# Edge counts of a graph network's scatter by a row DMA and ScalarE instead of TensorE transposes

## The chip, the cores and the metric

The kernel runs on one core of a Trainium2 chip. The metric is the device time of one execution in microseconds (us); shown for the kernel before are nine timed runs and one profiled execution. The engines are called as the profile calls them: PE (TensorE matmuls), PEld (TensorE weight loads), DVE (VectorE), ACT (ScalarE), POOL (GpSimd) and SP (SyncE, which here only issues DMAs).

## The reference

One layer of a message-passing network on 6250 nodes of 128 features and 100000 edges, the edges sorted by destination. All is f32.

```python
msg_in = jnp.concatenate([node_features[row], node_features[col]], axis=-1)
h = jax.nn.relu(msg_in @ Wm1 + bm1)
h = jax.nn.relu(h @ Wm2 + bm2)
messages = h @ Wm3 + bm3
agg = jax.ops.segment_sum(messages, col, num_segments=num_nodes)
count = jax.ops.segment_sum(jnp.ones((messages.shape[0],), messages.dtype), col, num_segments=num_nodes)
agg = agg / jnp.clip(count, 1.0)[:, None]
node_in = jnp.concatenate([node_features, agg], axis=-1)
upd = jax.nn.relu(node_in @ Wn1 + bn1) @ Wn2 + bn2
return node_features + upd
```

`row` is `src`, `col` is `dst`; the result is `_layernorm(x + layer(x))`. The count of edges that end in each node divides the sum.

## The kernel before, in words

**Tables (L335-L350).** The first layer is linear in the two gathered rows, so `x @ Wm1` is computed once a node and kept in DRAM: `atab` (source half, f32) and `btab` (destination half, as three bf16 terms whose sum is the f32 value). For each block of four 128-node tiles, `turn` transposes x on PE and copies it on ACT (L267), `a_table` multiplies (L232), copies (ACT L241) and stores by SP (L242). `b_table`, three blocks behind, multiplies, rounds on ACT (L249), subtracts on DVE (L250), rounds on POOL or, late, on ACT (L252, L254), subtracts again (L255) and stores (L256). At block 6 `starts` and at 7 and 8 `columns` make the edges' index columns. `x_part` makes `x @ Wn1` of the first half for the end (L316 to L320). SP, ACT and POOL each issue DMAs; the order of PE is the program's, that of DVE and ACT is the program's only from L368 until iteration 6 of the loop, and elsewhere the planner's, by priorities and its own costs.

**The loop over 196 groups of 512 edges (L532-L586).** At step i: `fetch` of group i (POOL issues four indirect DMAs that gather rows of `atab`, L412, into one of four `ag` buffers; SP issues four loads of `btab` rows, L418, into one of four `bw` buffers); every second step ACT issues two loads `db` of destinations (L361); DVE makes one-hot matrices `oht` and `oh` (L433, L436). Then PE does, in this order: `add_up` of group k = i-6 (six transposes L489), `first_layer` of group i-2 (16 transposes of `ag` L449, 8 matmuls of `bw` with `oht` L455, all into the two PSUM banks `ph`; ACT applies relu, L460), `sums` of group i-5 (L478; ACT copies the result `part` out of PSUM, L481), and `second_layer` of the group before (16 matmuls L469; DVE takes the max, L471).

**The counts.** `h2` has a 257th column of ones, so column 256 of `part` (a row is one of 4 x 32 window nodes) is the number of edges. `add_up` turns `part` over: per half of 64 rows, two transposes for the 256 features and a third (c = HC) whose weights are column 256 broadcast over 128 columns, so that the counts stand in all 128 partitions of a third plane of `pt`. Four DVE adds (L494) then put the three planes onto a window of `acc`, at a node that DVE loads into a register (L497).

**After the loop (L588-L601)** the last three groups are added up, in an order written out for PE, DVE and ACT, and then a loop for edges whose windows are too narrow (L607-L633), which runs no time with these inputs.

**Nodes (L636-L766).** For 15 blocks of up to 512 nodes: `products` (`w3` times `acc`, L672; DVE adds count times bias, L674; POOL multiplies by the reciprocal of the count, L677), `hidden` (L686 to L688), `moments` (L700 to L710), `scaled` (L733, L735). PE runs `products` four blocks ahead. For the first three blocks DVE makes the reciprocal from the counts in `acc` (L666, L667); for the others one row of counts goes by DMA to a column, is inverted (L654 to L656), goes to DRAM (`rtab`, L657) and comes back broadcast (L669).

Of the kernel before, what the change touches and what calls it, by code (L numbers as in the profile page):

```python
# [19 lines left out]
P = 128  # L20
EPS = 1e-5
NONE = 16384
WN = 32
# [4 lines left out]
def kernel(  # L28
# [74 lines left out]
    rtab = dram.tile([NT * P], F32, name="rtab")  # L103
# [47 lines left out]
    with tc.tile_pool(name="prep", bufs=1) as prep, tc.tile_pool(  # L151
# [9 lines left out]
        with tc.high_priority():  # L161
            nc.scalar.dma_start(w1, wm1.rearrange("(k p) h -> p k h", p=P))
            load_rows(nc.scalar, dst_i, dst)
            load_rows(nc.gpsimd, src_i, src)
            with nc.allow_non_contiguous_dma(reason="a bias, one value a partition"):
                nc.gpsimd.dma_start(b1, bm1.rearrange("(c p) -> p c", p=P))
                nc.gpsimd.dma_start(b2, bm2.rearrange("(c p) -> p c", p=P))
                nc.gpsimd.dma_start(b3, bm3.rearrange("(c p) -> p c", p=P))
                nc.gpsimd.dma_start(bu1, bn1.rearrange("(c p) -> p c", p=P))
            nc.gpsimd.dma_start(nb2[:, 0, :], bm2.rearrange("(o h) -> o h", o=1).to_broadcast([P, H]))  # L170
# [11 lines left out]
            nc.sync.dma_start(x_sb[:N - NTF * P, NTF, :], x[NTF * P:, :])  # L182
        nc.sync.dma_start(w2, wm2.rearrange("(k p) h -> p k h", p=P))
# [35 lines left out]
        order.enter_context(tc.manual_schedule(engines={ENG.PE}))  # L219

# [22 lines left out]

        def b_table(t0):
# [5 lines left out]
            nc.vector.tensor_sub(rest[:, :m], pbt[:, :m], bt[:, :m, 0])  # L250
            if t0 < 4 * LATE:
                nc.gpsimd.tensor_copy(bt[:, :m, 1], rest[:, :m])  # L252
            else:
                nc.scalar.copy(bt[:, :m, 1], rest[:, :m])  # L254
# [80 lines left out]
        turn(0)  # L335
        for i in range(BLOCKS + BEHIND):
            if i + 1 < BLOCKS:
                turn(4 * i + 4)
            if i < BLOCKS:
                for t0 in range(4 * i, min(4 * i + 4, NT), 2):  # L340
                    a_table(t0)
            if i == INDICES:
                starts()
            if i - INDICES in (1, 2):
                columns(i - INDICES - 1)
            if i >= BEHIND:
                for t0 in range(4 * (i - BEHIND), min(4 * (i - BEHIND) + 4, NT), 2):
                    b_table(t0)
            if BLOCKS - 1 <= i < BLOCKS - 1 + len(X_BESIDE):
                whole(x_part(X_BESIDE[i - BLOCKS + 1], bank_pb, (nc.scalar, nc.scalar)))  # L350
# [445 lines left out]
```

## Time and profile before

| what | us |
|---|---|
| median of nine runs (lowest, highest) | 1430.65 (1428.83, 1433.54) |
| the profiled execution, device time | 1433.35 |
| its span, first to last instruction | 1431.6 |
| busy: PE / PEld / DVE / ACT / POOL | 1247.8 / 917.9 / 661.8 / 452.9 / 805.2 |
| tables and indices, until the first L449 | 0 to 90 |
| the loop, first L469 to the last group's | 95 to 1346 |
| nodes, first L672 to the end | 1356 to 1432 |
| one loop step, median of first L469 to first L469 | 6.32 |

A row of the profile's groups reads: line, engine, operation, tiles written <- read, shape, how many, then busy time in us and mean ns of one, then the idle time of the engine just before them and what ended most of it. A row of the timeline reads: start, duration over all, engine, line, operation, how many, and in brackets the idle time before it and what ended it. The granted TensorE clock is 0.986 of full speed over the span. DMA engines are busy 80 to 90% in the first 70 us, 40 to 50% in the loop.

### The profile page before, as it was taken

The page shows a single profiled execution, that of the slowest core. Times are in us where ns is not written, and L with a number is a line of the kernel's source. Part 1 is how long each engine was busy: PE and PEld are TensorE (multiplying, and loading weights), DVE is VectorE, ACT ScalarE, POOL GpSimd, SP SyncE. Part 2 cuts the span into 40 slices and gives each one's busy share as a digit, 9 for nine tenths or more (in the row PEclk, how much of TensorE's full clock was granted, in tenths as well). Part 3 has the DMA queues.
Part 4 walks back from the last instruction along what each step waited for, and adds up shares of the span by engine and source line. Part 5 has one row for each costly group of instructions (what it writes and reads, how often), then busy time and mean ns, then how long its engine had stood idle before and what let it go on. Part 6 is the DMA issues. An engine that isn't in the chain of part 4 may idle for free. (4 is left out here: it accounts for less than half of the span.)

```text
span 1431.6 us, 32804 instructions
## 1 busy us (share of the span) xinstructions
PE 1247.8 (87%) x11196; PEld 917.9 (64%) x11197; DVE 661.8 (46%) x2083; ACT 452.9 (32%) x1160; POOL 805.2 (56%) x859
## 2 busy tenths in 40 slices
PE   7978888988888888888888898898888888888997
PEld 6646666666666666666666666666666666666656
DVE  5733444444443434444444444444444444443577
ACT  5632222232322323232233232222323233232246
POOL 7356565656556566565665665556565565655031
PEclk9989999999999999999999999999999999999999
DMA  8855555555444444444444444444444444443053
GB/s 282 293 168 144 148 162 145 152 148 152 126 128 122 120 129 127 124 118 124 131 127 124 130 120 124 126 123 122 120 129 124 127 122 120 130 121 107 15 142 111
DMA packets 173672, 193.66 MB, mean 135 GB/s; under 512 B 30844, under 2 KB 145486, under 8 KB 173488
## 3 DMA queue, kind: packets, MB, share of 16 engines
q0 software_dynamic: 37984, 103.35, 26.4%
q1 hardware_dynamic: 106956, 61.93, 14.7%
q10 hardware_dynamic: 28564, 26.27, 6.6%
q8 instruction: 90, 1.47, 0.4%
q14 instruction: 78, 0.64, 0.1%
HBM read 168.92 MB, written 22.88 MB: 134 GB/s over the span
## 5 line engine op out<-in xcount | busy, mean ns | idle before, releaser
L412 POOL DMA_INDIRECT ag<-atab,srcT x784 | 753.0, 961 | 505.8 <-PE ph L455 294.3
L469 PE MATMUL ph<-w,h 128*128 128x256 f32 x3128 | 734.5, 388 | 1.0 <-issue 1.0
L469 PEld LDWEIGHTS ph<-w,h 128*128 128x128 f32 x3128 | 583.0, 191 | 156.2 <-issue 67.1
L460 ACT ACTIVATE h<-ph,b 128x256 f32<-128x256 f32 x782 | 306.3, 474 | 900.1 <-PE ph L455 754.4
L471 DVE TENSOR_TENSOR h<-ph,nb 128x512 f32<-128x512 f32 x391 | 269.6, 692 | 671.0 <-PE ph L449 242.3
L455 PE MATMUL ph<-oht,bw 64*128 64x128 bf16 x1564 | 126.8, 217 | 146.6 <-issue 129.8
L494 DVE TENSOR_TENSOR acc<-acc,pt 128x63 f32 x782 | 172.8, 221 | 32.1 <-PE ph L455 2.5
L455 PEld LDWEIGHTS <-bw 64*128 64x128 bf16 x1564 | 67.0, 95 | 185.4 <-issue 157.6
L449 PE MATMUL ph<-ident,ag 64*128 64x64 f32 x3128 | 132.2, 223 | 10.3 <-DVE b L382 6.5
L478 PE MATMUL pg<-h,oh 128*32 128x257 f32 x1564 | 129.3, 394 | 4.1 <-issue 2.7
L449 PEld LDWEIGHTS ph<-ident,ag 64*128 64x128 f32 x3128 | 114.3, 139 | 10.8 <-DVE b L382 6.5
L433 DVE TENSOR_SCALAR oht<-db,pbase 128x128 bf16<-128x128 int32 x392 | 104.3, 296 | 4.7 <-remote 3.0
L489 PEld LDWEIGHTS pt<-ident,part 64*128 64x128 f32 x1173 | 51.1, 136 | 65.6 <-issue 64.2
L489 PE MATMUL pt<-ident,part 64*128 64x64 f32 x1173 | 77.9, 238 | 0.0
L481 ACT COPY part<-pg 128x257 f32<-128x257 f32 x196 | 76.6, 391 | 4.0 <-PE pg L478 4.0
L436 DVE TENSOR_TENSOR oh<-iota_n,dloc 128x128 f32<-128x128 f32 x196 | 55.7, 284 | 3.4 <-PE pg L478 2.7
L677 POOL TENSOR_TENSOR agg<-total,rc 128x512 f32<-128x512 f32 (+2 forms) x15 | 16.0, 1070 | 72.0 <-DMA rcol<-acc 34.3
L478 PEld LDWEIGHTS pg<-h,oh 128*32 128x32 f32 x1564 | 31.9, 108 | 30.9 <-issue 5.7
L232 PE MATMUL pbt<-w,xT 128*128 128x256 f32 x196 | 48.6, 393 | 2.7 <-ACT bt L241 1.8
L232 PEld LDWEIGHTS pbt<-w,xT 128*128 128x128 f32 x196 | 36.6, 196 | 11.0 <-ACT bt L241 3.0
L672 PE MATMUL pmt<-acc,w 128*128 128x512 f32 (+2 forms) x60 | 26.2, 576 | 2.3 <-DVE rc L666 2.3
L252 POOL CAST bt<-rest 128x512 bf16<-128x512 f32 x18 | 12.2, 686 | 27.1 <-DVE rest L250 18.1
(110 smaller groups left out, 421.4 us busy)
## 6 DMA issues: line engine op xcount, KB each, us to landing
bw<-btab SPq DMA_DIRECT2D x782, 32.0 KB
db<-in_dst_dram ACTq DMA_DIRECT2D x194, 128.0 KB
ag<-atab,srcT POOLq DMA_INDIRECT x784
btab<-bt SPq DMA_DIRECT2D x24, 384.0 KB
atab<-bt SPq DMA_DIRECT2D x24, 256.0 KB
xd<-in_x_dram SPq DMA_DIRECT2D x12, 256.0 KB
x2tab<-xd SPq DMA_DIRECT2D x12, 256.0 KB
x_sb<-in_x_dram SPq DMA_DIRECT2D x5, 512.0 KB
```

The costliest lines, as they stand in the source:

```text
L232: nc.tensor.matmul(pbt[:, a, :], xT[:, (t0 + a) * P:(t0 + a + 1) * P], w1[:, k, :], start=True, stop=True)
L412: nc.gpsimd.indirect_dma_start(out=ag[:, j, :], out_offset=None, in_=atab[:, :], in_offset=bass.IndirectOffsetOnAxis(ap=idx[:, j:j + 1], a ...
L433: nc.vector.tensor_scalar(oht[:n, k, :], db[:n, k * P:(k + 1) * P], pb_cols[:n, k:k + 1], None, op0=ALU.is_equal)
L449: nc.tensor.matmul(phs[h][:, c, u * NQ:(u + 1) * NQ], ag[halves[h], u, c * P:(c + 1) * P], ident[halves[h], halves[h]], is_transpose=True, ...
L455: nc.tensor.matmul(phs[h][:, c, k * P:(k + 1) * P], bw[halves[h], k, c * P:(c + 1) * P], oht[halves[h], k, :], start=False, stop=True, ski ...
L460: nc.scalar.activation(h1[:, c, h * 2 * P:(h + 1) * 2 * P], phs[h][:, c, :], AF.Relu, bias=b1[:, c:c + 1])
L469: nc.tensor.matmul(ph2[:, a, :], h1[:, c, (j0 + a) * P:(j0 + a + 1) * P], w2[:, c, :], start=(c == 0), stop=(c == HC - 1))
L471: nc.vector.tensor_tensor(h2[:, j0:j0 + 2, :H], ph2, nb2.to_broadcast([P, 2, H]), op=ALU.max)
L478: nc.tensor.matmul(pg[j * WN:(j + 1) * WN, :], oh[:, j, :], h2[:, j, :], start=True, stop=True, skip_group_check=True)
L481: nc.scalar.copy(part[:n, :], pg[:n, :])
L489: nc.tensor.matmul(pt[:, c, :], rows, ident[halves[h], halves[h]], is_transpose=True, start=True, stop=True, skip_group_check=True)
L494: nc.vector.tensor_add(window, window, pts[j // 2][:, :, k:k + WB])
```

## The change

Eight parts.

1. In the loop `add_up` makes only the two feature planes on PE (four transposes a group instead of six). `sums` has ACT issue a DMA from column 256 of `part` (128 partitions, 4 bytes each) to a row `row` in one partition; a step later than before (`k = g - lag - 2`) ACT copies this row into partition 0 of the third plane. `pt` becomes one tile of two banks, set to zero once. The counts now stand in partition 0 of `acc` alone.
2. The last four groups, not three, are added up behind the loop, and these still by three transposes a half.
3. In the node stage counts are broadcast: for the first three blocks by a matmul with ones (one contraction row) and an ACT copy, for the others by loading two rows of `rtab` (reciprocals, and the counts themselves, stored by one more DMA) instead of one. `rc` has four buffers instead of six, `u` three instead of four.
4. The loads of `dst`, `src` and the biases lose their priority over the loads of x, and `dst` goes to POOL's queue.
5. ACT's order in the table stage is the program's. The first `a_table` comes before the second `turn`.
6. The second half of the late `b_table`s (`b_terms`) comes one table behind.
7. The three early loads of `db` are issued in the last blocks of the table loop, and the x parts beside them go to ACT and DVE in turn.
8. The padded copy of `dst` in DRAM (`dpad`) is written after a small tile whose stretch it overlaps.

```diff
@@ -100,7 +100,7 @@
 ...
     dpad = dram.tile([NG * GE], I32, name="dpad")
-    rtab = dram.tile([NT * P], F32, name="rtab")
+    rtab = dram.tile([2, NT * P], F32, name="rtab")
     x2tab = dram.tile([NT * P, D], F32, name="x2tab")
@@ -160,14 +160,6 @@
 ...
             nc.scalar.dma_start(w1, wm1.rearrange("(k p) h -> p k h", p=P))
-            load_rows(nc.scalar, dst_i, dst)
-            load_rows(nc.gpsimd, src_i, src)
-            with nc.allow_non_contiguous_dma(reason="a bias, one value a partition"):
-                nc.gpsimd.dma_start(b1, bm1.rearrange("(c p) -> p c", p=P))
-                nc.gpsimd.dma_start(b2, bm2.rearrange("(c p) -> p c", p=P))
-                nc.gpsimd.dma_start(b3, bm3.rearrange("(c p) -> p c", p=P))
-                nc.gpsimd.dma_start(bu1, bn1.rearrange("(c p) -> p c", p=P))
-            nc.gpsimd.dma_start(nb2[:, 0, :], bm2.rearrange("(o h) -> o h", o=1).to_broadcast([P, H]))
 ...
@@ -180,6 +172,15 @@
 ...
             nc.sync.dma_start(x_sb[:N - NTF * P, NTF, :], x[NTF * P:, :])
+        load_rows(nc.gpsimd, dst_i, dst)
+        load_rows(nc.gpsimd, src_i, src)
+        with nc.allow_non_contiguous_dma(reason="a bias, one value a partition"):
+            nc.gpsimd.dma_start(b1, bm1.rearrange("(c p) -> p c", p=P))
+            nc.gpsimd.dma_start(b2, bm2.rearrange("(c p) -> p c", p=P))
+            nc.gpsimd.dma_start(b3, bm3.rearrange("(c p) -> p c", p=P))
+            nc.gpsimd.dma_start(bu1, bn1.rearrange("(c p) -> p c", p=P))
+        nc.gpsimd.dma_start(nb2[:, 0, :], bm2.rearrange("(o h) -> o h", o=1).to_broadcast([P, H]))
         nc.sync.dma_start(w2, wm2.rearrange("(k p) h -> p k h", p=P))
 ...
@@ -217,6 +218,8 @@
 ...
         order.enter_context(tc.manual_schedule(engines={ENG.PE}))
+        turns = ExitStack()
+        turns.enter_context(tc.manual_schedule(engines={ENG.Activation}))
@@ -241,6 +244,8 @@
 ...
+        unfinished = []
         def b_table(t0):
 ...
@@ -248,6 +253,13 @@
 ...
             nc.vector.tensor_sub(rest[:, :m], pbt[:, :m], bt[:, :m, 0])
+            unfinished.append((t0, m, bt, rest))
+            if len(unfinished) > 1 or t0 < 4 * LATE:
+                b_terms()
+        def b_terms():
+            t0, m, bt, rest = unfinished.pop(0)
             if t0 < 4 * LATE:
 ...
@@ -332,13 +344,28 @@
 ...
+        def destinations(g, ng, dst_row):
+            db = ld.tile([P, 2, 2 * P], I32, name="db", bufs=3)
+            if isinstance(g, int) and g < 6:
+                nc.vector.tensor_copy(db[:, 0, :1], srcT[:, 0, :1])
+            for h in range(2):
+                edges = dst_row[:, ds(g * GE, ng * GE)].rearrange("o (s e) -> o s e", s=ng)
+                edges = edges[:, :, h * 2 * P:(h + 1) * 2 * P]
+                nc.scalar.dma_start(db[h * NQ:(h + 1) * NQ, :ng, :], edges.to_broadcast([NQ, ng, 2 * P]))
+            return [db[:, k, :] for k in range(ng)]
+        dst_row = dst.rearrange("(o e) -> o e", o=1)
+        early = []
         turn(0)
         for i in range(BLOCKS + BEHIND):
-            if i + 1 < BLOCKS:
-                turn(4 * i + 4)
-            if i < BLOCKS:
-                for t0 in range(4 * i, min(4 * i + 4, NT), 2):
-                    a_table(t0)
+            tiles = range(4 * i, min(4 * i + 4, NT), 2) if i < BLOCKS else []
+            for n, t0 in enumerate(tiles):
+                if n == (i == 0) and i + 1 < BLOCKS:
+                    turn(4 * i + 4)
+                a_table(t0)
             if i == INDICES:
 ...
@@ -346,26 +373,14 @@
 ...
                     b_table(t0)
+            if BLOCKS - 3 <= i < BLOCKS:
+                early.append(destinations(2 * len(early), 2, dst_row))
             if BLOCKS - 1 <= i < BLOCKS - 1 + len(X_BESIDE):
-                whole(x_part(X_BESIDE[i - BLOCKS + 1], bank_pb, (nc.scalar, nc.scalar)))
-        def destinations(g, ng, dst_row):
-            db = ld.tile([P, 2, 2 * P], I32, name="db", bufs=3)
-            if isinstance(g, int) and g < 6:
-                nc.vector.tensor_copy(db[:, 0, :1], srcT[:, 0, :1])
-            for h in range(2):
-                edges = dst_row[:, ds(g * GE, ng * GE)].rearrange("o (s e) -> o s e", s=ng)
-                edges = edges[:, :, h * 2 * P:(h + 1) * 2 * P]
-                nc.scalar.dma_start(db[h * NQ:(h + 1) * NQ, :ng, :], edges.to_broadcast([NQ, ng, 2 * P]))
-            return [db[:, k, :] for k in range(ng)]
-        dst_row = dst.rearrange("(o e) -> o e", o=1)
-        early = [destinations(2 * k, 2, dst_row) for k in range(3)]
-        turns = ExitStack()
-        turns.enter_context(tc.manual_schedule(engines={ENG.DVE, ENG.Activation}))
+                whole(x_part(X_BESIDE[i - BLOCKS + 1], bank_pb, (nc.scalar, nc.vector)))
+        b_terms()
+        turns.enter_context(tc.manual_schedule(engines={ENG.DVE}))
         for b in X_BEHIND:
 ...
@@ -396,7 +411,7 @@
 ...
         name="pa", bufs=1, space=PSUM
-    ) as pa, tc.tile_pool(name="pt", bufs=2, space=PSUM) as ptp:
+    ) as pa, tc.tile_pool(name="pt", bufs=1, space=PSUM) as ptp:
@@ -470,28 +485,42 @@
 ...
-        def sums(oh, h2, nt):
+        def sums(oh, h2, nt, as_row=False):
 ...
                                  start=True, stop=True, skip_group_check=True)
-            part = wk.tile([P, H + 1], F32, name="part")
+            part = wk.tile([P, H + 1], F32, name="part", bufs=3)
             nc.scalar.copy(part[:n, :], pg[:n, :])
-            return part
+            if not as_row:
+                return part, None
+            row = wk.tile([1, P], F32, name="row", bufs=3)
+            nc.scalar.dma_start(row[:, :n], part[:n, H:])
+            return part, row
+        pts = ptp.tile([P, 2, 4 * P], F32, name="pt")
+        nc.vector.memset(pts, 0.0)
+        planes = [pts[:, h, :(HC + 1) * NQ].rearrange("p (c n) -> p c n", c=HC + 1) for h in range(2)]
         def add_up(part, firsts, nt):
-            pts = [ptp.tile([P, HC + 1, NQ], F32, name="pt") for _ in range(nt // 2)]
-            for c in range(HC + 1):
-                for h, pt in enumerate(pts):
+            part, row = part
+            for c in range(HC if row is not None else HC + 1):
+                for h in range(nt // 2):
                     rows = part[halves[h], c * P:(c + 1) * P] if c < HC else part[halves[h], H:].to_broadcast([NQ, P])
-                    nc.tensor.matmul(pt[:, c, :], rows, ident[halves[h], halves[h]], is_transpose=True,
+                    nc.tensor.matmul(planes[h][:, c, :], rows, ident[halves[h], halves[h]], is_transpose=True,
                                      start=True, stop=True, skip_group_check=True)
+            if row is not None:
+                nc.scalar.copy(pts[0:1, :nt // 2, HC * NQ:(HC + 1) * NQ],
+                               row[:, :nt * WN].rearrange("o (h n) -> o h n", n=NQ))
             for j, first in enumerate(firsts):
 ...
                 k = j % 2 * WN
-                nc.vector.tensor_add(window, window, pts[j // 2][:, :, k:k + WB])
+                nc.vector.tensor_add(window, window, planes[j // 2][:, :, k:k + WB])
 ...
@@ -534,10 +563,11 @@
 ...
                 late_loads()
-                none = wk.tile([16, (NG * GE - E) // 16], I32, name="none", bufs=1)
+                none = wk.tile([16, (NG * GE - E) // 16 + 1], I32, name="none", bufs=1)
                 nc.vector.memset(none, NONE)
+                nc.sync.dma_start(dpad[E - 16:].rearrange("(p e) -> p e", p=16), none)
                 nc.sync.dma_start(dpad[:E].rearrange("(p e) -> p e", p=16), dst.rearrange("(p e) -> p e", p=16))
-                nc.sync.dma_start(dpad[E:].rearrange("(p e) -> p e", p=16), none)
             for step, after in enumerate((20, 24, 27)):
 ...
@@ -561,7 +591,7 @@
 ...
                 oht = hots.pop(g)
-            k = g - lag - 1
+            k = g - lag - 2
             if 0 <= k < NG:
 ...
@@ -577,7 +607,7 @@
 ...
                 s = st[k]
-                s["part"] = sums(s["oh"], s["h2"], s["nt"])
+                s["part"] = sums(s["oh"], s["h2"], s["nt"], as_row=k < NG - lag - 1)
 ...
@@ -587,16 +617,18 @@
 ...
             rest = (p for b in X_END for p in x_part(b, bank_p1, (nc.scalar, nc.scalar)))
-            for k in range(NG - lag, NG):
+            lasts = range(NG - lag - 1, NG)
+            for k in lasts:
                 s = st[k]
 ...
             next(rest)
-            for k in range(NG - lag, NG):
+            for k in lasts:
                 s = st[k]
-                if k + 1 < NG:
+                if lasts[0] < k + 1 < NG and "part" not in st[k + 1]:
                     st[k + 1]["part"] = sums(st[k + 1]["oh"], st[k + 1]["h2"], st[k + 1]["nt"])
                 add_up(s["part"], s["firsts"], s["nt"])
-                next(rest)
+                if k > lasts[0]:
+                    next(rest)
             assert next(rest, None) is None
 ...
@@ -652,35 +684,40 @@
 ...
         nc.sync.dma_start(rcol, acc[0:1, HC, :NT * P].rearrange("o (p n) -> o p n", n=NC))
+        nc.sync.dma_start(rtab[1:2, :], acc[0:1, HC, :NT * P])
         nc.vector.tensor_scalar_max(rcol, rcol, 1.0)
         nc.vector.reciprocal(rcol, rcol)
-        nc.sync.dma_start(rtab.rearrange("(p n) -> p n", n=NC), rcol)
-        rrow = rtab.rearrange("(o n) -> o n", o=1)
+        nc.sync.dma_start(rtab[0:1, :].rearrange("o (p n) -> (o p) n", n=NC), rcol)
+        rrows = rtab.rearrange("(o k) n -> o k n", o=1)
 ...
             w = n1 - n0
-            rc = nd.tile([P, NB], F32, name="rc", bufs=6)
+            rc = nd.tile([P, 2, NB], F32, name="rc", bufs=4)
             if b < SELF:
-                nc.vector.tensor_scalar_max(rc[:, :w], acc[:, HC, n0:n1], 1.0)
-                nc.vector.reciprocal(rc[:, :w], rc[:, :w])
+                pct = pm.tile([P, NB], F32, name="pct", tag="pmt")
+                nc.tensor.matmul(pct[:, :w], ones[0:1, :], acc[0:1, HC, n0:n1], start=True, stop=True)
+                nc.scalar.copy(rc[:, 1, :w], pct[:, :w])
+                nc.vector.tensor_scalar_max(rc[:, 0, :w], pct[:, :w], 1.0)
+                nc.vector.reciprocal(rc[:, 0, :w], rc[:, 0, :w])
             else:
-                nc.sync.dma_start(rc[:, :w], rrow[:, n0:n1].to_broadcast([P, w]))
+                nc.sync.dma_start(rc[:, :, :w], rrows[:, :, n0:n1].to_broadcast([P, 2, w]))
             pmt = pm.tile([P, NB], F32, name="pmt")
 ...
             total = nd.tile([P, NB], F32, name="total", bufs=3)
-            nc.vector.scalar_tensor_tensor(total[:, :w], acc[:, HC, n0:n1], b23, pmt[:, :w],
+            nc.vector.scalar_tensor_tensor(total[:, :w], rc[:, 1, :w], b23, pmt[:, :w],
                                            op0=ALU.mult, op1=ALU.add)
             agg = nd.tile([P, NB], F32, name="agg", bufs=5)
-            nc.gpsimd.tensor_mul(agg[:, :w], total[:, :w], rc[:, :w])
+            nc.gpsimd.tensor_mul(agg[:, :w], total[:, :w], rc[:, 0, :w])
             return agg
 ...
             w = n1 - n0
-            u = nd.tile([P, HC, NB], F32, name="u", bufs=4)
+            u = nd.tile([P, HC, NB], F32, name="u", bufs=3)
             for c in range(HC):
 ...
```

More of the change, by code (lines that the diff above doesn't have):

```diff
@@ L333 @@
         assert sorted(X_BESIDE + X_BEHIND + X_FIRST + X_END) == list(range(BLOCKS))
-        turn(0)
-        for i in range(BLOCKS + BEHIND):
-            if i + 1 < BLOCKS:
-                turn(4 * i + 4)
-            if i < BLOCKS:
-                for t0 in range(4 * i, min(4 * i + 4, NT), 2):
-                    a_table(t0)
[L342 to L349, printed above, removed]
-                whole(x_part(X_BESIDE[i - BLOCKS + 1], bank_pb, (nc.scalar, nc.scalar)))
         def destinations(g, ng, dst_row):
@@ L364 @@
         dst_row = dst.rearrange("(o e) -> o e", o=1)
-        early = [destinations(2 * k, 2, dst_row) for k in range(3)]
-        turns = ExitStack()
-        turns.enter_context(tc.manual_schedule(engines={ENG.DVE, ENG.Activation}))
+        early = []
+        turn(0)
+        for i in range(BLOCKS + BEHIND):
+            tiles = range(4 * i, min(4 * i + 4, NT), 2) if i < BLOCKS else []
[3 more added lines that the diff above has]
+                a_table(t0)
+            if i == INDICES:
+                starts()
+            if i - INDICES in (1, 2):
+                columns(i - INDICES - 1)
+            if i >= BEHIND:
+                for t0 in range(4 * (i - BEHIND), min(4 * (i - BEHIND) + 4, NT), 2):
+                    b_table(t0)
+            if BLOCKS - 3 <= i < BLOCKS:
+                early.append(destinations(2 * len(early), 2, dst_row))
+            if BLOCKS - 1 <= i < BLOCKS - 1 + len(X_BESIDE):
+                whole(x_part(X_BESIDE[i - BLOCKS + 1], bank_pb, (nc.scalar, nc.vector)))
+        b_terms()
+        turns.enter_context(tc.manual_schedule(engines={ENG.DVE}))
         for b in X_BEHIND:
```

## The prediction

> **What bounds the kernel now.** I read the busy shares first, then the loop's timeline, then the stages by windows. PE is busy 87% of the span, so a change that takes transposes from PE looks like a gain. The groups price what is taken away:
>
> ```profile
> L412 POOL DMA_INDIRECT ag<-atab,srcT x784 | 753.0, 961 | 505.8 <-PE ph L455 294.3
> L489 PE MATMUL pt<-ident,part 64*128 64x64 f32 x1173 | 77.9, 238 | 0.0
> ```
>
> The loop takes 1250 of 1432 us, so one of its steps is looked at: PE alone, then POOL alone, in the middle of the loop.
>
> ```profile
> 628.22 3.72 PE L469 MATMUL ph<-w,h 128*128 128x256 f32 x16
> 631.87 0.40 PE L489 MATMUL pt<-ident,part 64*128 64x64 f32 x6
> 632.10 0.66 PE L449 MATMUL ph<-ident,ag 64*128 64x64 f32 x16
> 632.60 0.22 PE L455 MATMUL ph<-oht,bw 64*128 64x128 bf16 x1
> 633.68 0.38 PE L455 MATMUL ph<-oht,bw 64*128 64x128 bf16 x7 [0.87 <-issue]
> ...
> 627.98 0.95 POOL L412 DMA_INDIRECT ag<-atab,srcT  x1 [1.57 <-PE ph L455]
> 631.75 0.95 POOL L412 DMA_INDIRECT ag<-atab,srcT  x1 [0.30 <-issue]
> 634.28 0.95 POOL L412 DMA_INDIRECT ag<-atab,srcT  x1 [1.57 <-PE ph L455]
> ```
>
> PE stands still for 0.87 us inside L455, between two matmuls that need nothing new. It does so in nearly every step. In the last steps, where POOL gathers nothing more, it doesn't:
>
> ```profile
> 1334.06 0.39 PE L489 MATMUL pt<-ident,part 64*128 64x64 f32 x6
> 1334.29 0.66 PE L449 MATMUL ph<-ident,ag 64*128 64x64 f32 x16
> 1334.79 0.39 PE L455 MATMUL ph<-oht,bw 64*128 64x128 bf16 x8
> 1335.11 0.64 PE L478 MATMUL pg<-h,oh 128*32 128x257 f32 x8
> 1335.68 3.72 PE L469 MATMUL ph<-w,h 128*128 128x256 f32 x16
> ```
>
> The same work, dense, takes 5.27 us from one L469 to the next (1330.41 to 1335.68); in the middle of the loop the median is 6.32. DVE tells the same: in the last steps L471 begins 0.04 us after its last L469 matmul, in the middle 1.8 to 2.1 us after it. So something holds back PE and its signals by about 1 us a step while gathers run. What it is, this trace doesn't say, but its clock is POOL's: four gathers take 4.72 us (627.98 to 632.70); PE moves again 0.98 later (633.68); it finishes L455 and signals, and POOL restarts 0.60 after that. Sum 4.72 + 0.98 + 0.60 = 6.30, the whole step. A second look, where POOL was late once by 1.6 us:
>
> ```profile
> 236.96 0.97 POOL L412 DMA_INDIRECT ag<-atab,srcT  x1 [3.20 <-issue]
> 240.76 0.96 POOL L412 DMA_INDIRECT ag<-atab,srcT  x1 [0.30 <-issue]
> 242.96 0.95 POOL L412 DMA_INDIRECT ag<-atab,srcT  x1 [1.24 <-remote]
> ```
>
> PE then ran one step dense (L469 at 235.79, then 241.06), and the next took 8.32 (249.38): three steps together 20.2 instead of 19.0, though four buffers of gathered rows lie between the two engines. A delay of POOL reaches PE almost whole. I take the loop as bound by this lockstep, with PE some 0.9 us a step ahead of it.
>
> The stages by windows (time, then busy time of PE, PEld, DVE, ACT, POOL, then clock, DMA share, GB/s):
>
> ```profile
> 0.00:24.00 24.00, 15.61 (x69) 12.60 (x70) 12.78 (x26) 11.41 (x16) 21.89 (x39) 1.00 0.94 291
> 48.00:67.00 19.00, 16.67 (x70) 11.99 (x69) 13.02 (x21) 13.12 (x24) 5.71 (x9) 1.00 0.94 330
> 1355.90:1363.00 7.10, 7.07 (x17) 4.84 (x18) 6.37 (x10) 0.00 (x0) 1.30 (x3) 0.57 0.28 61
> ```
>
> The tables are bound by DMA (share 0.94), the node stage by PE, which leads the chain of waits from 1356 to 1421 and starts at a clock of 0.57.
>
> **The loop, part 1.** Removed: two of six transposes in 192 steps. Six take 0.18 us in the dense step (1334.06 to the first weight load of L449 at 1334.24), so two take 0.06: 11.5 us in all if PE decided. They lie ahead of the 0.87 us stall, which then grows by 0.06. I take **0**; the low end is -11.5.
>
> Added on ACT's queue, one DMA a step of 128 packets of 4 bytes. The trace has no such DMA. The nearest row is `db`: two issues, 128 packets each of about 1 KB, every second step, on the same queue. Steps 5 to 189, counted by whether they hold such a pair: 94 without, mean 6.32 us; 91 with, mean 6.51. So 0.19 for a pair, 0.094 an issue, 18.0 us in 192 steps as the upper end. The lower end is nothing, since the row is wanted a whole step later and ACT is idle 4.5 us a step. Between them I scale by the packets' cost: on SP's queue (14.7% of 16 engines' span over 106956 packets) one takes 31.5 ns, on ACT's (6.6% over 28564) 52.9; small packets are nearer SP's. 0.094 x 31.5/52.9 = 0.056, times 192 = **+10.8**.
>
> The Trainium skill speaks against this DMA: "DMA: Bandwidth & Descriptors", section "Rules for kernel authors", says that a last dimension that isn't contiguous is broken into one descriptor per element and advises to rearrange it. No run here shows that; by it the row costs as many descriptors as one `db` load has packets, and the loop's term would be 18.0 and the time 1448.
>
> ACT's new copy (one partition, 128 values; L481 with 257 takes 0.39) and L494, which now waits for it, cost **0**: the adds may come up to 2.5 us later, in DVE's idle time ahead of L471 (2.56 us in that step). Behind a late copy on ACT stand relu L460 and then L469 of the next step, 3 us off. If that cover went, 0.3 us a step. The adds run a step later with nothing behind them but the same bank's next transposes, a step away. SP's loads of `bw` share completion signals with ACT's DMAs and may wait for the row, but lie three steps ahead: 0. `dpad`'s copy (391 KB) now runs in the loop: 0, or 1.1 by its bytes at 352 GB/s.
>
> **Tables, parts 4 to 8.** The loop's start hangs on `atab`: its last store is issued at 63.47, POOL begins at 66.97, gathers 16 times without pause until 87.52, and DVE gets PE's signal for L382 only at 89.77; L449 follows at 89.98. So the loop starts 23 us after `atab`, as long as PE's last x part (83.4) isn't later. `dpad` leaves the saturated stretch (-1.1); the first `a_table` needn't wait for the second `turn` (9.71 against the copy's end at 7.26, -2.4); `dst` leaves the hardware queues, where SP waited 9 us for earlier loads before its first store at 16.42. Against it: `dst` comes later on POOL, but the index chain has 11 us in hand (21.5 to 32.6), and ACT, in program order, may wait where the planner found other work. `b_terms` and the x parts work on `btab`, off this path: 0. I take **-3.5**, ends -7 and +2.
>
> **Behind the loop, part 2.** One more group, 0.2 us of PE and 1.05 of DVE, while PE computes x parts and waits: **0**, at most +1.
>
> **Nodes, part 3.** Three broadcasts of counts, each two passes of 106, 256, 256 columns; a 256-column pass takes 0.215 (L686, four in 0.86): 1.04 us at full clock, 1.8 at 0.57, on the chain: +1.8. DVE's L674 now waits for the load of `rc`, which is twice as large; before, POOL's L677 alone waited for it, 4.4 us in two waits. Behind L674 on DVE stand L687 and L705, and behind these PE. I take +0.7 of 0 to 4.4. Together **+2.5**, ends +1.0 and +6.2.
>
> **Sum.** 10.8 - 3.5 + 0 + 2.5 = +9.8. The profiled execution is 1433.35 (span 1431.6 and 1.75 around it), 2.7 above the median of the runs; against the median, 1430.65 + 9.8 = **1440**. The forecast's own range is 1434 to 1448.
>
> **Rivals.**
> *A, PE decides the loop after all.* For it: PE busy 87%, POOL idle 1.57 a step on PE's signal. Against it: the late POOL step. -11.5 - 3.5 + 2.5 = -12.5: 1418. It holds if the stall is PE's own and keeps its length.
> *B, the row lies in a trough.* Gathers come in bursts, DMA is busy only 0.47 of the loop, and the row's 512 bytes are wanted a step later. Against it: `db`, which has three such steps of time too, still costs 0.19. 0 - 3.5 + 2.5 = -1.0: 1430.
> *C, the row costs as much as a `db` issue, and `rc` reaches PE.* 18.0 - 3.5 + 6.2 = +20.7: 1451. It decides where a step's hold-up follows the number of descriptors.
> That the transposes aren't removed can be excluded: L489 must fall to 789.
>
> **Numbers.** Forecast 0.40, A 0.25, B 0.20, C 0.15. A measurement tells from no change about 0.2%, 2.9 us, 1427.8 to 1433.5. Of B 0.06 falls below, 0.10 within, 0.04 above: faster 0.31, same 0.10, slower 0.59. The range, 1417 to 1453, takes in the middles of A and C.
>
> **What would show it.** The step's median near 6.37 with the stall in L455 near 0.95: the lockstep and the row's price. A median of 6.26 with the stall unchanged: A. First L449 near 86.5; L672's first block to the end near 78.5 us. I am wrong at the root if the step without `db` and that with it no longer differ, or if PE's stall vanishes though gathers go on.

## The result, and the profile after

The changed kernel takes **1439.36 us** (median of ten runs, 1435.47 to 1441.38), the kernel before 1430.54 in the runs beside it: ratio 1.0057, 95% interval 1.0046 to 1.0068, so 8.2 us (6.6 to 9.7) slower. The forecast was 1440, 9.8 slower. The sum was near; most of its terms were not, and they cancelled, so that the nearness is in good part luck. The traces show it first (us; a second trace of the kernel before was taken later):

| | before | before, second trace | after |
|---|---|---|---|
| first L469 (L484 after) | 95.1 | 93.4 | 98.8 |
| first to last of them | 1250.4 | 1248.1 | 1243.5 |
| last of them to the first node matmul | 10.4 | 10.5 | 12.4 |
| first node matmul to the end | 75.7 | 74.3 | 84.4 |

The loop, which was to lose 10.8, gained. Tables and nodes, for which 1 us less was forecast, take 12.5 more than in the first trace (98.8 for 95.1, 84.4 for 75.7). The groups of the profile after show that the change does what it says: the transposes fall from 1173 to 789, and ACT has a copy a group.

```profile
L427 POOL DMA_INDIRECT ag<-atab,srcT x784 | 750.2, 957 | 504.9 <-PE ph L470 310.6 <-issue 180.8 <-DMA db<-in_dst_dram 5.8
L515 PE MATMUL pt<-ident,part 64*128 64x64 f32 x789 | 66.4, 247 | 1.5 <-DVE acc L523 1.4
L518 ACT COPY pt<-row 1x128 f32<-1x128 f32 x192 | 49.7, 259 | 817.4 <-PE ph L464 547.7 <-DMA db<-in_dst_dram 135.4 <-DMA row<-part 47.9
```

A step in the middle of the loop, from the timeline of the changed kernel (its L464, L470, L484 are L449, L455, L469 of before):

```profile
629.21 0.61 ACTq L356 DMA_DIRECT2D db<-in_dst_dram  x1
630.12 0.95 POOL L427 DMA_INDIRECT ag<-atab,srcT  x1 [0.31 <-issue]
630.26 0.34 PE L515 MATMUL pt<-ident,part 64*128 64x64 f32 x4
...
630.93 0.27 PE L470 MATMUL ph<-oht,bw 64*128 64x128 bf16 x3
631.54 0.21 PE L470 MATMUL ph<-oht,bw 64*128 64x128 bf16 x1 [0.33 <-issue]
632.25 0.29 PE L470 MATMUL ph<-oht,bw 64*128 64x128 bf16 x4 [0.50 <-issue]
...
632.78 0.95 POOL L427 DMA_INDIRECT ag<-atab,srcT  x1 [1.71 <-PE ph L470]
```

PE still stands still inside the layer of `bw`, 0.83 us here in two pieces, between matmuls that need nothing new, and POOL restarts 1.71 us after its fourth gather. The lockstep of the prediction is there. Over steps 5 to 189 PE's idle time a step grew from 0.80 or 0.81 in the two traces of before to 0.86, by about the 0.06 that the two transposes had taken.

The nodes, from the timeline of the changed kernel (L701 and L709 are the matmuls of `products`, L711 to L714 its DVE and POOL work, L723 that of `hidden`):

```profile
1354.71 0.47 PE L701 MATMUL pct<-acc,ones 1*128 1x106 f32 x2 [2.31 <-issue]
...
1361.05 0.41 DVE L689 RECIPROCAL rcol<-rcol 128x49 f32<-128x49 f32 x1
...
1361.49 0.36 SPq L690 DMA_DIRECT2D rtab<-rcol  x1
...
1363.57 1.38 SPq L706 DMA_DIRECT2D rc<-rtab  x3
...
1373.96 0.16 DVE L763 RECIPROCAL rs<-sd 106x1 f32<-106x1 f32 x1 [1.25 <-ACT sd L754]
1374.16 0.16 DVE L765 SCALAR_TENSOR_TENSOR sh<-mv,rs 106x1 f32<-106x1 f32 x1
1374.24 2.06 DVE L711 SCALAR_TENSOR_TENSOR total<-rc,b,pmt 128x512 f32<-128x512 f32 x3
...
1375.07 3.72 POOL L714 TENSOR_TENSOR agg<-total,rc 128x512 f32<-128x512 f32 x3 [10.07 <-DVE total L711]
...
1376.39 3.63 PE L723 MATMUL put<-agg,wu 128*128 128x512 f32 x4 [2.83 <-POOL agg L714]
```

Read it from below. PE waits 2.83 us for the fourth block's `agg`; POOL waits for `total`; `total` stands on DVE directly behind L763 and L765, which belong to block 0's normalisation and wait for ACT. And the granted clock, by windows (the number after POOL's):

```profile
1356.00:1358.00 2.00, 2.00 (x5) 1.17 (x5) 1.31 (x3) 0.37 (x1) 0.41 (x1) 0.50 0.02 2
...
1364.00:1366.00 2.00, 2.00 (x6) 1.12 (x5) 0.34 (x2) 0.00 (x0) 0.72 (x1) 0.50 0.86 207
1366.00:1368.00 2.00, 2.00 (x7) 1.04 (x6) 0.39 (x2) 0.59 (x2) 0.00 (x0) 0.98 0.74 174
...
1376.00:1378.00 2.00, 1.60 (x2) 0.84 (x3) 0.31 (x1) 0.00 (x0) 2.00 (x3) 0.58 0.66 143
```

PE ran at half its clock for 10.24 us from 1355.85 on, and for 3.41 us again after the wait.

### The profile page after: what moved, and what is told of

It reads as the page before. It is cut to its first block, busy times and chain, and to the rows that moved or that the text cites. A ratio compares the mean times of both kernels' runs of the same rounds, so it can differ in the third digit from the quotient of the medians.

```text
span 1439.2 us, 32129 instructions
## 1 busy us (share of the span) xinstructions
PE 1239.7 (86%) x10818; PEld 908.5 (63%) x10819; DVE 660.8 (46%) x2087; ACT 500.5 (35%) x1352; POOL 802.4 (56%) x862
## 3 DMA queue, kind: packets, MB, share of 16 engines
q0 software_dynamic: 38160, 103.75, 27.2%
## 5 line engine op out<-in xcount | busy, mean ns | idle before, releaser
L484 PE MATMUL ph<-w,h 128*128 128x256 f32 x3128 | 732.2, 387 | 0.0
L484 PEld LDWEIGHTS ph<-w,h 128*128 128x128 f32 x3128 | 581.6, 191 | 153.7 <-issue 69.7
L518 ACT COPY pt<-row 1x128 f32<-1x128 f32 x192 | 49.7, 259 | 817.4 <-PE ph L464 547.7
L470 PE MATMUL ph<-oht,bw 64*128 64x128 bf16 x1564 | 130.0, 217 | 168.8 <-issue 154.0
L470 PEld LDWEIGHTS <-bw 64*128 64x128 bf16 x1564 | 69.3, 95 | 206.8 <-issue 195.5
L464 PE MATMUL ph<-ident,ag 64*128 64x64 f32 x3128 | 130.5, 223 | 2.8 <-PE ph L484 1.4
L464 PEld LDWEIGHTS ph<-ident,ag 64*128 64x128 f32 x3128 | 113.5, 139 | 4.4 <-issue 4.1
L515 PEld LDWEIGHTS pt<-ident,part 64*128 64x128 f32 x789 | 39.6, 137 | 67.6 <-issue 65.8
L515 PE MATMUL pt<-ident,part 64*128 64x64 f32 x789 | 66.4, 247 | 1.5 <-DVE acc L523 1.4
L714 POOL TENSOR_TENSOR agg<-total,rc 128x512 f32<-128x512 f32 (+2 forms) x15 | 16.0, 1071 | 82.4 <-DVE rc L704 42.8
L723 PE MATMUL put<-agg,wu 128*128 128x512 f32 (+2 forms) x60 | 25.7, 554 | 2.8 <-POOL agg L714 2.8
```

The lines of the kernel that those rows point to most:

```text
L464: nc.tensor.matmul(phs[h][:, c, u * NQ:(u + 1) * NQ], ag[halves[h], u, c * P:(c + 1) * P], ident[halves[h], halves[h]], is_transpose=True, ...
L470: nc.tensor.matmul(phs[h][:, c, k * P:(k + 1) * P], bw[halves[h], k, c * P:(c + 1) * P], oht[halves[h], k, :], start=False, stop=True, ski ...
L484: nc.tensor.matmul(ph2[:, a, :], h1[:, c, (j0 + a) * P:(j0 + a + 1) * P], w2[:, c, :], start=(c == 0), stop=(c == HC - 1))
L515: nc.tensor.matmul(planes[h][:, c, :], rows, ident[halves[h], halves[h]], is_transpose=True, start=True, stop=True, skip_group_check=True)
```

## The experiments

The theory from these traces: the row costs little, the loop gains, and tables, tail and nodes lose; its rival is the prediction's own sum. Twelve runs were made, the first of them the kernel before again. The first eight fell on chips on which the kernel before takes 1429 to 1430 us, the last four on chips on which it takes 1208. Each ratio is against runs of the kernel before on the same chip.

**The parts one by one.** First the kernel before once more, for its trace.

> The kernel before, unchanged, for a second trace of it. In the first trace its loop held five long steps (7.2 to 8.9 us, together about 8 us over the median step), and the changed kernel's had none; the loop's gain there was 6.9 us (1250.4 to 1243.5, first to last L469). If the long steps belong to the kernel before, this trace has four to six of them again and a loop near 1250. If they are an accident of one execution, their number and places differ, and the loop lies anywhere from 1243 to 1251: then the gain of the loop is not shown by the two traces.

The long steps came again at the same places: 22, 75, 128, 129 and 180 or 181, with 8.9 and 10.5 us over the median step in all. They belong to the kernel.

`tables_only`: the kernel before with the change's hunks of the tables, the loads and `dpad` (parts 4 to 8), as in the diff above.

> The kernel before with parts 4 to 8 alone (order of loads, of the copies on ACT and of the tables). By the two traces (first L469 at 95.1 before, 98.8 after) +3.7 us, about 1434, with the loop and the nodes as before. By the prediction -3.5, about 1427. If the late loop start comes only of the other parts (the new tiles, another plan), 1430.5.

0.9983 (0.9971 to 0.9995), -2.4 us. The traced start was late all the same (first L469 at 99.1), and the gain lay in the loop, where no such long step remained: behind the first steps, which are long in every trace, the only one over 7 us took 7.08. Both expectations were half right.

`loop_only`: the kernel before with parts 1 and 2. `loop_no_row` takes this away from it:

```diff
-            row = wk.tile([1, P], F32, name="row", bufs=3)
-            nc.scalar.dma_start(row[:, :n], part[:n, H:])
-            return part, row
+            return part, True
...
-            if row is not None:
-                nc.scalar.copy(pts[0:1, :nt // 2, HC * NQ:(HC + 1) * NQ], ...)
```

> The kernel before with parts 1 and 2 alone. The node stage is the one before and reads the counts from all partitions, where only partition 0 holds them, so the mean and the bias are left out of most of the output; its work is the same. By the prediction (row +10.8, transposes 0) 1441. If the row's DMA costs next to nothing and two transposes fewer let the step shorten by what the traces show in the median (0.015 to 0.04 a step, 3 to 8 us) with 1 to 2 us given back behind the loop, 1424 to 1429. If the gain of the loop was an accident of the one trace, 1430 to 1433.

> As the one with parts 1 and 2 alone, but without the row's DMA and ACT's copy: in the loop the counts are not made at all (the third plane stays zero). Against that kernel it gives the price of the row. By the prediction 10.8 us less than with the row, and equal to the kernel before (transposes worth 0): 1430 to 1432. If the row is nearly free, it is within 2 us of the kernel with the row. If PE decided (rival A), 11.5 below the kernel before, 1419 to 1421.

`loop_only` 1.0021 (1.0010 to 1.0032), +3.0; `loop_no_row` 0.9983 (0.9971 to 0.9996), -2.4. So the row, its DMA together with ACT's copy and the adds' wait for it, costs 5.4 us (by the two intervals some 3 to 8), about half of what was forecast and not nothing. Which of the three makes the price is open. The medians of the steps agree: with a `db` pair 6.476 without the row and 6.495 with it, without a pair 6.221 and 6.244; by the sum of steps 5 to 189 the row adds 9.9, of which 3.1 lie in the long steps; but the two traced executions, of 1437.7 and 1422.4 us, are the slowest and the fastest of their twelve, so the price is taken from the ratios. Both kernels take 10.8 us from the start of the very last L469 matmul to the nodes, where the kernel before takes 8.8: the tail costs 1.9. Most of it is one wait, here from the timeline of the changed kernel, where the transposes of a group stand until DVE has added up the one before:

```profile
1347.47 0.40 PE L515 MATMUL pt<-ident,part 64*128 64x64 f32 x6 [1.39 <-DVE acc L523]
```

Hence the two transposes are worth -2.4 - 1.9 = -4.3.

`no_nodes`: the changed kernel with part 3 undone.

> The changed kernel with part 3 undone: its node stage is that of the kernel before and reads the counts from all partitions, where only partition 0 holds them (mean and bias are left out of most of the output, the work is the same). If the parts add up (parts 4 to 8 alone -2.4, parts 1 and 2 alone +3.0), it takes +0.6 against the kernel before, and part 3 costs the other 7 to 8 us of the change. By the prediction's term for the nodes it takes 2.5 us less than the changed kernel. If the late stretch from the last L469 to the end (96.8 us in the changed kernel's trace, 84 to 88 in the others) belongs to the loop's new tail, it keeps 95 us or more.

1.0003 (0.9992 to 1.0014), +0.4: the parts add up (-2.4 + 3.0 = +0.6), and part 3 costs 8.2 - 0.4 = **7.8 us** (by the two intervals some 5.6 to 10). Its nodes, from the timeline:

```profile
1364.47 0.59 PE L718 MATMUL put<-agg,wu 128*128 128x106 f32 x4
1364.75 0.75 DVE L706 SCALAR_TENSOR_TENSOR total<-acc,b,pmt 128x512 f32<-128x512 f32 x1 [0.38 <-PE pmt L704]
...
1366.63 2.50 POOL L709 TENSOR_TENSOR agg<-total,rc 128x512 f32<-128x512 f32 x2 [1.46 <-DMA rc<-rtab]
```

The fourth block's `total` waits for PE alone, POOL alone for `rc`, and PE never stands.

**What in the nodes costs it.** Two kernels, each the changed one with one edit:

```diff
 total_no_wait
-            nc.vector.scalar_tensor_tensor(total[:, :w], rc[:, 1, :w], ...
+            nc.vector.scalar_tensor_tensor(total[:, :w], rc[:, 1, :w] if b < SELF else acc[:, HC, n0:n1], ...
 no_pct
-                nc.tensor.matmul(pct[:, :w], ones[0:1, :], acc[0:1, HC, n0:n1], start=True, stop=True)
-                nc.scalar.copy(rc[:, 1, :w], pct[:, :w])
-                nc.vector.tensor_scalar_max(rc[:, 0, :w], pct[:, :w], 1.0)
+                nc.vector.tensor_scalar_max(rc[:, 0, :w], acc[:, HC, n0:n1], 1.0)
```

(`no_pct` also lets `total` of these blocks read `acc`.)

> The changed kernel, but DVE's total (L711) of the blocks behind the third takes the counts from acc in place of the loaded row, so it no longer waits for the load of rc; the load keeps its size. The bias is left out of these blocks in all partitions but the first. If the nodes' extra time comes of that wait (PE stands 2.83 us for the fourth block's agg and then runs 3.6 us at half its clock), 5 to 7 us less than the changed kernel, near 1432 to 1434. If it comes of the pct matmuls and the chain on DVE behind them, at most 2 us less. By the prediction's term for this wait: 0.7 us less.

> The changed kernel without the pct matmuls: for the first three blocks DVE takes counts from acc as in the kernel before (wrong but in partition 0, so mean and bias are left out there); rc's load and DVE's wait for it stay. By the prediction 1.8 us less than the changed kernel. If the pct matmuls delay DVE's work on rcol, and with it the store of rtab, the loads of rc and the wait at the fourth block, 4 to 6 us less. If only the wait by itself counts, 1 to 2 less.

`total_no_wait` 1.0041 (1.0025 to 1.0057), `no_pct` 1.0042 (1.0028 to 1.0056): each about 2 us less than the changed kernel, with intervals that overlap its own, so the times alone don't show that either edit helps. In the traces the node stage falls from 84.4 to 79.5 without the wait (PE no longer stands; the half clock still lasts 10.24) and to 77.9 without `pct` (no half clock at the start; the stand of 2.82 remains), and it is 75.8 with neither. Up to some 2 us of the fall to 77.9 can be the phase of the clock, since kernels with the node stage of before take 73.6 to 75.8 there by how many stretches at half clock they meet. By the traces each has a share, and neither is the whole. One thing more: `rc`'s load was issued later into the stage in `total_no_wait` (9.7 us against 8.9), and yet its `agg` ran 15.1 us in, where the changed kernel's `total` ran only 19.5 us in. So the changed kernel's `total` did not wait for the data at the last, but for its place in DVE's order, behind L763 and L765. `no_pct` shows the same from another side: its `rc` is loaded 5.6 us into the stage, as before (5.5), and yet the fourth block's `total`, which waits for `rc` there too, runs 12.9 us in, where the kernel before has it at 7.3. DVE isn't idle ahead of it, and PE stands behind it:

```profile
1367.79 1.41 DVE L707 SCALAR_TENSOR_TENSOR total<-rc,b,pmt 128x512 f32<-128x512 f32 x2
1369.94 3.19 PE L719 MATMUL put<-agg,wu 128*128 128x512 f32 x4 [2.82 <-POOL agg L710]
```

`pct_full` gives `pct` all rows of the array:

```diff
-                nc.tensor.matmul(pct[:, :w], ones[0:1, :], acc[0:1, HC, n0:n1], start=True, stop=True)
+                nc.tensor.matmul(pct[:, :w], ones, acc[:, HC, n0:n1], start=True, stop=True)
```

> The changed kernel with pct's matmuls over all 128 partitions of ones and acc in place of partition 0 alone (the counts of the last groups' nodes stand in all partitions, so there the count comes out 128 times too large); columns and passes are the same. Both traces with pct over one partition have PE's clock at 0.50 for three stretches of 3.41 us at the start of the nodes, those without pct none, one or two. If one row of the array is too little work to bring the clock back, full rows leave one or two stretches, and the time falls by 1 to 3 us against the changed kernel (1439.4). If the pct matmuls cost by their time and by what they delay on DVE, it stays within 1 us, with three stretches.

It fell on a chip of 1208 us, so its time (ratio 0.9975, 0.9962 to 0.9988) can't stand beside the changed kernel's. It shows something else: the whole change, but for the rows of `pct`, is 3.0 us faster there than the kernel before. The changed kernel itself did not run on such a chip. Its trace has two stretches of half clock at the start of the nodes, where both traces with one row have three. One trace and a phase that differs from run to run: it fits the theory of the one row and doesn't settle it. PE's stand of 2.82 us was there too.

`tables_warm` has PE work on before the nodes:

```diff
+            fill = pa.tile([P, H + 1], F32, name="pg")
+            for _ in range(6):
+                nc.tensor.matmul(fill[:, :H], ident, w2[:, 0, :], start=True, stop=True)
         order.close()
```

> The kernel before with parts 4 to 8, and six matmuls of 256 columns behind the last group that nothing reads, so that PE isn't idle for the 2.3 us ahead of the nodes. All traces have PE's granted clock at 0.50 for one, two or three stretches of about 3.4 us at the start of the nodes. If PE's idleness ahead of the nodes is what lowers the clock, it stays at 1.00 there and the time falls by 1.7 to 3.4 us against the same kernel without them (1426.4): 1423 to 1425. If the loop of no turns behind the last group waits for these matmuls, or the clock falls anyway, 1426 to 1429.

0.9997 (0.9987 to 1.0007), some 2 us more than `tables_only` by the two ratios, whose intervals overlap: a miss. Its expectation says that all traces have the clock at 0.50 at the start of the nodes; that was wrong too, since `tables_only` has no such stretch there, with PE idle for 2.32 us ahead. The idle time was not filled but moved. PE stands 2.27 us behind the six matmuls as it stood 2.32 without them, the time from the start of the last L469 matmul to the nodes grew from 8.83 to 11.37, and the clock fell for one stretch. Something at the loop of no turns holds PE after its last matmul, whenever that is; what, the trace doesn't show.

**The long steps.** In all traces with the old tables from the chips of 1430 us POOL pauses some 3 us (2.9 to 3.3, in place of 1.57) behind the fourth gather of groups 25, 78, 131 and 184, 53 apart; the late POOL step that the prediction shows (3.20, `issue`) is the first of them. With the new tables the pause has moved. `tables_only`, POOL's timeline at group 52:

```profile
408.55 0.95 POOL L427 DMA_INDIRECT ag<-atab,srcT  x1 [1.79 <-PE ph L470]
410.06 0.95 POOL L427 DMA_INDIRECT ag<-atab,srcT  x1 [0.56 <-issue]
```

0.56 in place of 0.30 between its first and second gather, the same at 105 and 158, and at no other place. Two edits to the kernel before should tell what places it: `shift_ops` and `shift_dma`.

```diff
 shift_ops
+    spare = const.tile([1, 2], F32, name="spare")
+    for k in range(2):
+        nc.gpsimd.memset(spare[:, k:k + 1], 0.0)
 shift_dma
+            spare = prep.tile([P, 1], I32, name="spare")
+            nc.gpsimd.dma_start(spare, dst[:P].rearrange("(p o) -> p o", o=1))
```

> The kernel before with two memsets of one element more on POOL, early, that nothing reads. In all traces with the tables of before, POOL pauses about 3.0 us in place of 1.57 behind the fourth gather of groups 25, 78, 131 and 184, and PE's step then takes 8 to 9 us; with the tables of the change (four more records on POOL ahead of the loop) it pauses 0.56 in place of 0.30 between the first and the second gather of groups 52, 105 and 158, and no such long step is seen. If it is the place in POOL's sequence of instructions that decides, two instructions move the pauses between two gathers, the four long steps are gone, and the time falls by 5 to 8 us, to 1423 to 1426. If the long steps come of where dst is loaded, or of other parts of the tables, they stay at the same groups and the time is that of the kernel before, 1429 to 1431.

> The kernel before with one more DMA issued by POOL ahead of the tables, which loads 128 values into 128 partitions that nothing reads. Two memsets more on POOL left its long pauses at groups 25, 78, 131 and 184, so a count of POOL's instructions does not place them. If what POOL's DMAs have written before places them (the tables of the change give POOL three DMAs more), 128 packets, as many as a gather has rows, move the pause to another gather: it then stands between two gathers and the long steps are gone; on a chip where steps take 6.3 us the time falls by 5 to 8 us, to 1423 to 1426, on one where PE runs dense, at 5.27 a step, by nothing. If neither places them, the pauses stay at these groups and the time is that of the kernel before within 2 us, or more where a cast on DVE happens to wait for POOL's memsets, as in the run with two memsets.

Two memsets left the pauses at 25, 78, 131 and 184 (1.85 to 2.01 in place of a usual 0.53 on this chip). One DMA moved them to 52, 105 and 158, 0.56 each, exactly as with the new tables. So something that POOL's earlier DMAs bring along places the pause, and the change most likely moved it by loading `dst` on POOL. By which rule stays open. It isn't the count of packets: the one load, whose expectation counted on 128, adds 32 to POOL's queue (37984 to 38016), the three loads of `dst` with the new tables 176 (38160), and both put the pause at the same gather. What the move is worth could not be timed here, since on these chips a late POOL costs PE nothing: `shift_dma` 1.0005 (0.9996 to 1.0014). `shift_ops` 1.0060 (1.0043 to 1.0077) lost 7 us to something else. Its trace shows a cast on DVE, 0.90 us in the kernel before, that took 12.45 while POOL's memsets of `acc` ran, and the loop then starts at 95.8, where `shift_dma` has 90.5. First the kernel before, then `shift_ops`:

```profile
7.24 15.80 POOL L376 MEMSET acc<- 128x784 f32 x21
10.39 0.90 DVE L190 CAST dst_f<-dst_i 98x1024 f32<-98x1024 int32 x1 [6.96 <-DMA dst_i<-in_dst_dram]
...
7.30 14.60 POOL L379 MEMSET acc<- 128x784 f32 x21
10.00 12.45 DVE L193 CAST dst_f<-dst_i 98x1024 f32<-98x1024 int32 x1 [6.57 <-DMA dst_i<-in_dst_dram]
```

In both kernels the cast runs beside the memsets, and only in one does it stand until they are over; what decides, these runs don't show.

`row_on_sp` issues the row from SP in place of ACT:

```diff
-            nc.scalar.dma_start(row[:, :n], part[:n, H:])
+            nc.sync.dma_start(row[:, :n], part[:n, H:])
```

> The kernel with parts 1 and 2 alone, but the row's DMA is issued by SP in place of ACT. With the row on ACT it took 1432.8, with no row 1426.1, and the median step with a db pair went from 6.476 to 6.495, without one from 6.221 to 6.244. If the row costs by standing with db in ACT's queue, SP's queue takes the price away: 1426 to 1428. If it costs as a DMA of 128 packets in any queue, or through the adds that wait for it, it stays near 1432. If SP, which waits in order, now holds up the loads of bw behind the wait for part, it is above 1436.

0.9912 (0.9896 to 0.9928), -10.6 us, which answers another question than it was asked. On these chips PE's stall isn't there at all. The kernel before, with two memsets more (`shift_ops`; its line numbers are three higher):

```profile
604.19 0.96 POOL L415 DMA_INDIRECT ag<-atab,srcT  x1 [0.30 <-issue]
604.51 0.40 PE L492 MATMUL pt<-ident,part 64*128 64x64 f32 x6
604.61 0.69 DVE L474 TENSOR_TENSOR h<-ph,nb 128x512 f32<-128x512 f32 x1 [1.03 <-PE ph L472]
604.74 0.66 PE L452 MATMUL ph<-ident,ag 64*128 64x64 f32 x16
...
605.24 0.39 PE L458 MATMUL ph<-oht,bw 64*128 64x128 bf16 x8
605.56 0.64 PE L481 MATMUL pg<-h,oh 128*32 128x257 f32 x8
605.68 0.95 POOL L415 DMA_INDIRECT ag<-atab,srcT  x1 [0.53 <-PE ph L458]
```

The layer of `bw` runs in one piece, PE has no idle time in the median step, DVE's max starts 0.03 us after PE's last matmul (600.86 + 3.72), POOL restarts after 0.53, and the median step is 5.274. With four transposes and the row it is 5.211: 0.063 a step, 12.1 us in 192 steps, less 1.9 for the tail, is 10.2, within the interval of the gain measured (8.7 to 12.6). That is the loop of rival A (-11.5), on a chip where its condition holds. SP's queue is no part of it: `pct_full`, whose row ACT issues, has the same median step of 5.211 and a loop of 1019.7 us, `row_on_sp` 1020.1. Whether SP's queue is cheaper for the row where the lockstep rules stays open.

## Why the prediction came out right, point by point

| term | predicted (ends) | measured |
|---|---|---|
| the row's DMA | +10.8 (0 to 18.0) | +5.4, with ACT's copy: `loop_only` less `loop_no_row` |
| two transposes | 0 (-11.5 to 0) | -4.3: `loop_no_row`, less the tail |
| behind the loop | 0 (at most +1) | +1.9, in every trace with part 2 |
| tables, loads | -3.5 (-7 to +2) | -2.4: `tables_only` |
| nodes | +2.5 (+1.0 to +6.2) | +7.8: changed kernel less `no_nodes` |
| sum | +9.8 | +8.4; the changed kernel +8.2 |

The term of the nodes is itself a difference from the changed kernel, so the last row tests only that the other terms add up (+0.6, and `no_nodes` +0.4).

- **The root held, on the chips it was read from.** PE's stall stayed and grew by 0.06, steps with and without `db` still differ (6.496 and 6.248), rival A's 1418 did not come. The step's median, forecast near 6.37, stayed at 6.30. That the transposes "lie ahead of the stall" and so give nothing was too strong: about a third of their 11.5 us came through (4.3, with an interval of some 2.5 to 6).
- **The row** was priced by the nearest row, half way up its bounds, and cost half of that. The packets' cost by which it was scaled was too high: a packet of 4 bytes on ACT's queue took 9.3 ns in `loop_only`, not 31.5; by 9.3 the same sum gives 3.2. The rule of the Trainium skill that the prediction weighed there ("DMA: Bandwidth & Descriptors", "Rules for kernel authors") speaks of one descriptor per element, and the count agrees: ACT's queue has 27648 packets more in `loop_only` than in `loop_no_row`, 144 for each of 192 rows of 128 values. The price that the prediction worked out from that count, 18.0, did not come: the queue's share of the 16 engines rose only from 6.5% to 7.3%.
- **Tables: the size was right and the reason wrong.** "First L449 near 86.5" came true (85.96), but it was only a transpose made early; the loop's first L469 came 3.7 us later, not 3.5 earlier. The index chain did not have its 11 us in hand. DVE's cast of `tilei` took 0.55 us before, and 3.68 in every kernel with the new tables, beside eight memsets of `acc` that POOL now runs just then. From the timelines of the changed kernel:

```profile
33.35 5.60 POOL L391 MEMSET acc<- 128x784 f32 x8
...
35.68 3.68 DVE L299 CAST tilei<-base 1x784 int32<-1x784 f32 x1
...
41.86 2.07 PE L235 MATMUL pbt<-w,xT 128*128 128x256 f32 x4 [2.83 <-DVE groups_i L308]
...
66.57 0.45 SPq L245 DMA_DIRECT2D atab<-bt  x1
...
71.16 1.35 POOL L427 DMA_INDIRECT ag<-atab,srcT  x1 [5.85 <-DMA db<-in_dst_dram]
```

  The cast ends 0.42 us after the memsets (39.36 and 38.94), `groups_i` comes late behind it and PE waits 2.83 us. The last store of `atab` is issued 3.1 us later than before, POOL's first gather starts 4.2 later, and the loop 3.7: it does hang on `atab`, as the prediction said. That the cast is the cause of the late store is read from this order and not shown by a run of its own. What paid for it were the four or five long steps, 9 to 10 us by the two traces of the kernel before, which are gone in every trace with the new tables, most likely by `dst`'s loads on POOL. The prediction had even shown one of them, as evidence of the lockstep, without asking where it came from or whether the change would touch it.
- **Behind the loop** the term was "PE waits anyway". It did not: with the fourth group PE's transposes wait for DVE's adds, 1.39 of the 1.9 us.
- **Nodes: the failing step.** The 1.8 us for `pct` counted its passes at the clock of before; they took 2.8 at a clock of 0.50. It didn't count that the stage would stay longer at half clock, nor that L703 and L704 on DVE, now behind `pct`, delay `rcol`, `rtab` and `rc`'s load (rc issued 8.9 us into the stage, before 5.5). And DVE's wait was given 0.7 of 4.4, by "behind L674 stand L687 and L705"; the order that the planner made for a `total` that waits for a DMA put it behind block 0's normalisation, and PE stood 2.83. Why the planner did so isn't shown. The whole stage, forecast near 78.5 us, took 84.4. What the prediction was right in is that this is where `rc` reaches PE. How the 7.8 us divide between `pct` and the wait stays open.

Of the two kernels of the diff neither is the best on the chips of 1430 us: `tables_only` beats both (-2.4 us against the kernel before and, by the two ratios, some 10 against the changed one). A version of it whose memsets don't meet the cast was not tried.

## What to carry to other kernels

Ask of every irregularity in a trace, one late step of fifty too, what places it, and whether the change moves that: by the traces the long steps that went add up to 9 or 10 us, more than any term of the sum. When a value that was computed in place comes by DMA instead, follow the in-order engine that now waits for it, and what the planner then puts ahead. And a sum that comes out right proves none of its terms; undoing one part at a time does.

## What the hardware showed that was not expected

- The same kernel takes 1430 us on some chips and 1208 on others, and nearly the whole difference is the loop (1250 us in the kernel before, 1031 in `shift_ops` and `shift_dma`; the kernel before itself has no trace there): PE's matmuls, POOL's gathers (0.96 us) and the gathers' packets (4096 bytes in 235 ns and in 230) take the same; what is gone is the time in which PE's matmuls and its signals to DVE, ACT and POOL are held back while gathers run. The cause wasn't found. Here the removal of PE's work was worth a third of its price on the one and all of it on the other.
- PE's clock falls to 0.50 in stretches of 3.41, 6.83 or 10.24 us, once of 13.65. The node stage of before's form takes 73.6 us with none at its start (`tables_only`), 74.3 with one, 75.5 to 75.8 with two. "TensorE: Matmul & The Clock Gate" of the Trainium skill, Part 1, has the activity window of about 3.4 us that runs freely; these traces agree, and show how many windows are lost varying from run to run of one kernel (6.83 and 3.41 us in the two traces of the kernel before).
- A cast on DVE can stand until a run of POOL's memsets beside it is over: 12.45 us in place of 0.90, and 3.68 in place of 0.55. Running beside them isn't enough: in the kernel before the cast took its 0.90 us amid 21 of them.
